# Two cross-attention layers in one kernel: an inverse root by Newton steps in place of a power, and a split issued two thirds of a slot earlier

## The chip, the cores and the metric

The kernel runs on one core of one Trainium2 chip. The metric is the device time of one execution in microseconds (us). The core has TensorE (PE in the profile, with its weight loads on a row of their own, PEld), VectorE (DVE), ScalarE (ACT), GpSimd (POOL) and SyncE (SP), which here only issues DMAs. Every engine works through its own queue in order.

## The reference

Sixteen sequences x of 256 positions by 320 channels pass through two cross-attention layers with 20 heads of 16 channels, against a context of 256 tokens by 512 channels. Both layers have text tokens, and a few image tokens whose attention gets an extra semantic term. The part of the second layer that the change touches:

```python
probs_t = jax.nn.softmax(scores_t, axis=-1)                    # text attention
qsem = jnp.einsum('bhst,bte->bhse', probs_t, text_ehs)         # mean text per head and position
qsem = _l2norm(qsem)                                           # x / max(|x|, 1e-12)
ip_n = _l2norm(ip_ehs)                                         # the 4 image tokens
sem = jnp.einsum('bhse,bne->bhsn', qsem, ip_n)
fused = attn_scores + 0.5 * sem
probs_ip = jax.nn.softmax(fused, axis=-1) * spatial_mask
ip_out = jnp.einsum('bhsn,bhnd->bhsd', probs_ip, v_ip)
out = (text_out + ip_out) @ W_out + b_out + residual
```

So for each position and head an inverse norm of `qsem` is wanted: 256 x 20 values in each batch.

## The kernel before

Everything is one unrolled program. It runs in *slots*: one slot is one group of four heads of one batch, five slots make a batch, slots 0 to 79 are layer 1 and slots 80 to 159 layer 2 (`NS` is 80). `slot1(k)` lists what TensorE does in a slot of layer 2, in order: scores and turned scores (`both1`: L894, L888), attention over the values (`attend1`: L948, and L958 for the norms), and the four steps of the norm's quadratic form (`norm1`: L936) of the slot before. Between them, at 0.33, 0.67 and 1.0 of the slot, `fill` runs side tasks whose due times have come. Each side task is a Python generator; the list of due times at its definition says at which slot each of its steps may be issued.

Matrices are split into a rounded high part and a low part, so that fast matmuls keep full precision. Four users of POOL matter here:

- `rounded1` (L926 on ACT, L927 on POOL): per slot four times, ACT rounds half of the attention weights P and POOL subtracts, 128 x 512 each. The result `wt` is multiplied by the norm's matmul (L937 on DVE) and summed by TensorE.
- `open1(b)`, with `split` and `project`: loads layer 1's output x of batch b (a DMA on SP into `xq`, one buffer), splits it (ACT L593 and L594, then POOL L595 and L596, tile `hq`, one buffer) and projects it to layer 2's queries (TensorE L606 and L609). The first matmul of L606 reads ACT's part, the second one reads POOL's. `open1(b)` has six due times relative to the batch's first slot n: load, split, then projection and its stores.
- `image_softmax(b)`: from the sums of `settle1` it makes the inverse norm (L1021, L1023, and the power at L1026, on POOL), the image scores (L1029, L1031), their maximum (L1034), exponential (L1038) and normalisation (L1044, L1046), then turns them over on DVE (L1053). `close1(b)` multiplies the result with the image values (TensorE L1063), and projects the output with its own split (tile `ho`, L595) and L606. For the last batch `image_softmax` runs in two parts: groups 0 to 3 (32 values per partition) and group 4 (8 values).
- `keys1` and `tokens1`: the split of the next context (L163) and small copies.

TensorE's order is pinned: it is the order in which the Python code issues matmuls. The other queues are ordered by a planner, which simulates the program with prices of its own and takes ready instructions by the order in which they were issued. `queued` adds a tie: the instruction isn't placed ahead of the last one that `anchor` marked on its engine. On ACT the anchors are the exponentials (L908), on POOL the subtractions (L927); the split of x (`hq`) is tied to both.

```python
    def queued(inst, *behind):
        for other in behind or [anchors.get(inst.ins.engine)]:
    ...
            anchor(nc.gpsimd.tensor_sub(W[k, u][:, t], P[k, u][:, t], f(R[k, u][:, t])))
    ...
        order = queued if tag == "hq" else lambda inst: inst
        order(eng.tensor_sub(hl[:, 3:5], src[:, 0:2], f(hl[:, 0:2])))
```

Of the kernel before, what the change touches and what calls it, by code (L numbers as in the profile page):

```python
# [11 lines left out]
ALU = mybir.AluOpType  # L12
# [9 lines left out]
CP = 384  # L22
# [8 lines left out]
NG = H // 4  # L31
# [11 lines left out]
def RAMP(t):  # L43
    return t if t < -5 or t > 3 else (t + 5) * 0.375
# [5 lines left out]
def xattn2(  # L50
# [27 lines left out]
    nc = tc.nc  # L78
    f = lambda ap: ap.bitcast(F32)
    mm = nc.tensor.matmul  # L80

    def dma(out, in_):
        nc.sync.dma_start(*(f(ap) if ap.dtype == FR else ap for ap in (out, in_)))
# [9 lines left out]
    whole = ps.tile([128, 1024], F32, tag="S0", name="S", bufs=1)  # L93
# [16 lines left out]
    def buf(tag, shape, dtype=F32, bufs=1, name=None):  # L110
        if tag in ("wB", "wD", "vr", "raw"):
            return sb.tile(shape, dtype, tag=tag, name=name or tag, bufs=bufs)
        size = 1
        for d in shape[1:]:
            size *= d
        if tag not in slots:
            slots[tag] = [0, dtype] + [const_tile([128, max(size, words.get(tag, 0))], f"{tag}_{i}", dtype) for i in range(bufs)]
        n, kind, *ring = slots[tag]
        assert kind == dtype and len(ring) == bufs, tag
        slots[tag][0] += 1  # L120
        t = ring[n % bufs][: shape[0], :size]
        names = "abcd"[: len(shape) - 1]
        if len(names) > 1:
            t = t.rearrange(f"p ({' '.join(names)}) -> p {' '.join(names)}", **dict(zip(names, shape[1:])))
        return t
# [305 lines left out]
    w1, v1t, gmt = {}, [], []  # L431
# [74 lines left out]
    def weights3():  # L506
        gm = buf("vr", [128, 3 * (H * V0W + 16)], FR, bufs=3, name="gm")
        gm = gm[:, : 7 * 128].rearrange("p (g n) -> p g n", n=128)
        nc.gpsimd.memset(f(gm), 0.0)
        gmt.append(gm)  # L510
        yield
        if len(gmt) == 2:
            one, two = [buf("rs", [128, 2 * S], bufs=2, name="one") for i in range(2)]
            w1["vb"], w1["mhalf"] = one[:, :CP], one[:, CP : CP + NG * 8]
            w1["pT"], w1["pip"] = two[:, :S], two[:, S:].rearrange("p (f c) -> p f c", c=32)
            nc.vector.memset(w1["mhalf"], -0.5)
            nc.gpsimd.memset(w1["pip"], 0.0)

    ct1, doubled = {}, {}
# [69 lines left out]
    def split(src, neg, eng, tag):  # L589

        hl = buf(tag, [128, 5, S], FR)
        order = queued if tag == "hq" else lambda inst: inst
        order(nc.scalar.copy(hl[:, 0:2], src[:, 0:2]))  # L593
        order(nc.scalar.activation(hl[:, 2], src[:, 2], AF.Copy, scale=neg))  # L594
        order(eng.tensor_sub(hl[:, 3:5], src[:, 0:2], f(hl[:, 0:2])))  # L595
        order(eng.tensor_add(hl[:, 2], src[:, 2], f(hl[:, 2])))  # L596
        return hl
# [15 lines left out]
    def queries(l, a):  # L613
        qh = buf("q", [128, 2, 3, S], FR)

        def evac(m, pp):
            evacuate(qh[:, 0, m], qh[:, 1, m], pp, m)

        qd = dram.tile([3, CH, S], F32, tag=f"qd{l}", name=f"qd{l}", bufs=2)
        steps = project(l, wq[l], a, evac)  # L620
        for m in range(2):
            next(steps)
            yield
        for r, s in ((0, 0), (1, 1), (2, 0)):
            dma(qd[r, :256].rearrange("(m p) t -> p m t", p=128), qh[:, s, :2])
        next(steps)
        for r, s in ((slice(0, 3, 2), 0), (slice(1, 2), 1)):
            to = qd[r, 256:].rearrange("r p t -> p r t")
            dma(to, qh[:64, s, 2].unsqueeze(1).to_broadcast(list(to.shape)))
        yield  # L630
        return qh, qd
# [4 lines left out]
    def load(src, tag):  # L636
        x = buf(tag, [128, 3, S])
        dma(x, src.rearrange("(k p) t -> p k t", p=128))
        return x
# [372 lines left out]
    def image_softmax(b, lo=0, hi=NG):  # L1012

        gs, n = slice(lo, hi), hi - lo
        nt, si = norms[b][:, gs], image[b]
        square = norms[b][:, lo + 1 : hi + 1, :, 5]
        pool = nc.gpsimd
        small = lambda n, t: buf(t, [128, NG, 8] + ([n] if n > 1 else []))[:, gs]

        u = small(1, "u")  # L1020
        pool.tensor_mul(u, nt[:, :, :, 0], nt[:, :, :, 0])  # L1021
        yield
        nc.vector.scalar_tensor_tensor(u, u, EPS2 / 4, square, op0=ALU.mult, op1=ALU.max)  # L1023
        yield
        r = small(1, "r")
        pool.tensor_tensor(r, u, w1["mhalf"].rearrange("p (f s) -> p f s", f=NG)[:, gs], op=ALU.pow)  # L1026
        b4 = lambda t: t.unsqueeze(3).to_broadcast([128, n, 8, NIP])
        a = small(NIP, "a")
        pool.tensor_mul(a, nt[:, :, :, 1:5], b4(r))  # L1029
        by_group = lambda t: t[:, :, : NG * NIP].rearrange("p f (g n) -> p g f n", n=NIP)[:, gs]  # L1030
        pool.tensor_add(a, a, by_group(si))  # L1031
        yield
        m4 = small(1, "m4")
        nc.vector.tensor_reduce(m4, a, axis=AX.X, op=ALU.max)  # L1034
        yield
        pool.tensor_sub(a, a, b4(m4))
        yield
        nc.scalar.activation(a, a, AF.Exp, scale=SCALE)  # L1038
        yield
        z4 = small(1, "z4")  # L1040
        nc.vector.tensor_reduce(z4, a, axis=AX.X, op=ALU.add)
        nc.vector.reciprocal(z4, z4)
        yield
        pool.tensor_mul(z4, z4, mk.unsqueeze(1).to_broadcast([128, n, 8]))  # L1044
        pi = w1["pip"]
        pool.tensor_mul(by_group(pi), a, b4(z4))  # L1046
        if hi < NG:
            return
        vb = w1["vb"]
        dma(vb, vipd[NIP * b : NIP * (b + 1)].unsqueeze(0).to_broadcast([32, NIP, CP]))  # L1050
        yield
        pT = w1["pT"]
        nc.vector.transpose(pT, pi.rearrange("p f c -> p (f c)"))  # L1053
        nc.gpsimd.tensor_mul(vb, vb, w1["bmask"])
        return pT, vb

    def close1(b):
        hT, (pT, bd) = results["gathered", 1, b], get("i1", b)

        def extra(hT):  # L1060
            for p in range(3):
                ip = bank()[:, :S]
                mm(ip, bd[:, p * 128 : (p + 1) * 128], pT, start=True, stop=True)  # L1063
                nc.vector.tensor_add(hT[:, p], hT[:, p], ip)
                yield

        y = yield from finish(1, b, hT, load(x1d[b], "xc"), extra)
        dma(out_d[b].rearrange("(k p) t -> p k t", p=128), y)
# [5 lines left out]
    def open1(b):  # L1074
        x = load(x1d[b], "xq")
        yield
        xs = split(x, tmask[:, 5:6], nc.gpsimd, "hq")
        yield
        get("w2")
        qh, qd = yield from queries(1, xs)  # L1080

        return qd
# [4 lines left out]
    def task(key, times, make, *needs):  # L1087
        tasks[key] = [times, 0, make, needs, len(tasks)]
# [14 lines left out]
    def get(*key):  # L1103
        while key not in results:
            step(key)
        return results[key]
# [20 lines left out]
    def shifted(n, *times):  # L1127

        return [RAMP(n + t) for t in times]
# [4 lines left out]
    for c in range(B // 2):  # L1134
        n, k = 10 * c, [("k0", c)] if c else []
# [11 lines left out]
    for b in range(B):  # L1147
        n = NS + 5 * b
        task(("k1", b), shifted(n, -7, -6.67, -6.33, -5.67, -5, -4.67), lambda b=b: keys1(b), ("w2",), *([("grams", b - 1)] if b else []), *([("w4", 1)] if b > 2 else []))
        task(("t1", b), shifted(n, -3.67, -3, -2.67, -2.33, -1.67), lambda b=b: tokens1(b), ("k1", b), ("w3", b % 2))  # L1150
        task(("o1", b), shifted(n, -7.67, -7, -6.67, -5.33, -4.33, -4), lambda b=b: open1(b), ("w7",), ("c0", b), *([("o1", b - 1)] if b else []))
        task(("i1", b), shifted(n, 6.67, 6.67, 6.67, 7.33, 7.33, 7.67, 7.67, 8, 8.33), lambda b=b: image_softmax(b, NG - 1 if b == B - 1 else 0), ("gathered", 1, b), ("taken", B + b - 1), *([("i1a",)] if b == B - 1 else []))
        task(("c1", b), shifted(n + (1.67 if b > B - 3 else 0), 8.67, 8.67, 8.67, 8.67, 9, 10.33, 11.67, 12.67), lambda b=b: close1(b), ("i1", b), ("w4", 1))
    task(("i1a",), [2 * NS + 0.1], lambda: image_softmax(B - 1, 0, NG - 1), ("i1", B - 2))
    spread = lambda t, d, n: [t + d * i for i in range(n)]
    thirds = lambda n, t: [t + i // 3 + (0.2, 0.6, 1.0)[i % 3] for i in range(n)]
# [4 lines left out]
    for i in range(2):  # L1161
        task(("w3", i), [NS - 4 + 5 * i], weights3)
# [147 lines left out]
```

## Time and profile before

| what | value |
|---|---|
| runs | 1537.6, 1539.21, 1541.0 us; median 1539.21 |
| profiled execution | 1533.3 us, of which the span from first to last instruction is 1531.5 |
| granted TensorE clock, mean | 0.982 |
| PE busy | 1439.7 us, 94% |
| POOL busy | 1263.5 us, 83% |
| DVE busy | 1116.6 us, 73% |
| ACT busy | 891.0 us, 58% |
| HBM traffic over the span | 127 GB/s |

Shares are means over two layers with different work. Layer 2 fills about the second half of the span; its batches repeat every 49.9 us. In timeline rows the first number is the start in us from the beginning of the span and the second the time that the group took; "x4" is the number of instructions, and brackets hold the engine's idle time before it and what ended it. L numbers are lines of the kernel.

### The profile page before, as it was taken

Reading aid. Unit: us, or ns where it says so; the run is one execution under the profiler, and the core shown is the slowest. Engines: PE = TensorE matmul, PEld = TensorE weight load, DVE = VectorE, ACT = ScalarE, POOL = GpSimd, SP = SyncE. Lnnn points to the kernel's source line nnn. Section 1 sums busy time; section 2 is a strip of 40 time slices with the busy share of each in tenths; the row PEclk is TensorE's granted clock in tenths of the full one; section 3 lists DMA queues with packets and bytes.
Section 4 is the critical chain, followed back from the end, with each engine's and each line's share of the span. In section 5 each row is a group of like instructions: output and inputs, shape, how many; then the busy total and the mean of one; then the engine's idle time right before and its main releaser. Section 6 shows DMA issues by size and latency. Waiting matters only on the chain.

```text
span 1531.5 us, 36088 instructions
## 1 busy us (share of the span) xinstructions
PE 1439.7 (94%) x12726; PEld 1162.6 (76%) x12726; DVE 1116.6 (73%) x2544; ACT 891.0 (58%) x2037; POOL 1263.5 (83%) x1325
## 2 busy tenths in 40 slices
PE   6789999999999999779999999999999999999996
PEld 5678878788888877657777777877777777777764
DVE  5466767676767677876787878777777877787874
ACT  5346555556565645545666666666656666666561
POOL 4269898889898986888688898888988898889796
PEclk9899999999999999999999999999999999999998
DMA  6766677677767675774444354444444344433311
GB/s 209 205 194 185 206 196 215 185 220 193 213 189 211 188 217 141 196 223 147 108 133 125 111 144 111 116 129 124 118 119 133 112 125 120 134 111 110 105 28 36
DMA packets 228815, 233.04 MB, mean 152 GB/s; under 512 B 38410, under 2 KB 198508, under 8 KB 228620
## 3 DMA queue, kind: packets, MB, share of 16 engines
q1 hardware_dynamic: 226428, 229.44, 53.0%
q8 instruction: 101, 1.65, 0.5%
q10 hardware_dynamic: 2208, 1.30, 0.3%
q14 instruction: 78, 0.64, 0.1%
HBM read 118.04 MB, written 77.10 MB: 127 GB/s over the span
## 4 chain that ended last, share of the span: by engine, by line
PE 69%; POOL 11%; DMA 8%; DVE 5%; ACT 3%; issue 2%; SPq 1%; ACTq 1%; POOLq 0%; DVEq 0%
PE X L936 14%; PE X L248 13%; PE X L606 6%; PE P L796 5%; PE P L948 4%; POOL wt L927 4%; PE S L739 4%; PE P L958 4%; PE T L763 3%; PE T L888 3%; PE S L894 3%; DMA ks<-M 2%; POOL P L769 2%; PE X L258 2%; PE X L609 2%
## 5 line engine op out<-in xcount | busy, mean ns | idle before, releaser
L769 POOL TENSOR_TENSOR P<-P,rs 128x512 f32<-128x512 f32 x320 | 408.1, 1299 | 91.3 <-ACT P L766 89.8
L927 POOL TENSOR_TENSOR wt<-P,ctb 128x512 f32<-128x512 f32 x320 | 405.8, 1292 | 68.1 <-ACT ctb L926 68.1
L936 PE MATMUL X<-ctb,gm 128*128 128x512 f32 x1120 | 305.3, 402 | 0.1
L766 ACT ACTIVATE P<-T 128x512 f32<-128x512 f32 x320 | 175.6, 594 | 151.1 <-PE T L763 107.9
L937 DVE TENSOR_TENSOR wt<-X,wt 128x512 f32<-128x512 f32 x320 | 216.7, 683 | 39.3 <-PE X L936 32.8
L908 ACT ACTIVATE P<-T 128x512 f32<-128x512 f32 x320 | 173.4, 594 | 80.0 <-PE T L888 77.5
L936 PEld LDWEIGHTS X<-ctb,gm 128*128 128x128 f32 x1120 | 196.1, 189 | 31.2 <-DVE wt L937 0.7
L926 ACT ACTIVATE ctb<-P 128x512 fp32r<-128x512 f32 x320 | 187.5, 627 | 22.9 <-PE X L936 21.7
L896 DVE TENSOR_REDUCE mn<-S 128x4 fp32r<-128x1008 f32 x160 | 191.6, 1197 | 0.0
L741 DVE TENSOR_REDUCE mn<-S 128x4 fp32r<-128x716 f32 x160 | 142.6, 891 | 0.0
L796 PE MATMUL P<-P,vr 128*32 128x256 f32 x1920 | 125.5, 391 | 4.7 <-POOL P L769 3.3
L739 PE MATMUL S<-ks,qs 125*128 125x256 f32 x640 | 117.2, 306 | 6.0 <-DMA qs<-tph 3.4
L739 PEld LDWEIGHTS S<-ks,qs 125*128 125x128 f32 x640 | 88.2, 194 | 40.9 <-issue 24.0
L1026 POOL TENSOR_TENSOR r<-u,rs 128x40 f32<-128x40 f32 (+2 forms) x17 | 108.8, 6397 | 3.9 <-DVE u L1023 3.8
L763 PE MATMUL T<-qs,ks 127*128 127x256 f32 x640 | 107.9, 290 | 4.0 <-ACT P L766 3.9
L740 DVE TENSOR_REDUCE mn<-S 128x4 fp32r<-128x308 f32 x160 | 74.4, 465 | 30.0 <-PE S L739 28.9
L763 PEld LDWEIGHTS T<-qs,ks 127*128 127x128 f32 x640 | 90.5, 194 | 7.3 <-ACT P L766 6.3
L796 PEld LDWEIGHTS P<-P,vr 128*32 128x32 f32 x1920 | 55.8, 111 | 46.2 <-issue 6.4
L606 PE MATMUL X<-hq,wE 128*128 128x256 f32 x512 | 80.6, 297 | 10.6 <-POOL hq L595 6.0
L807 DVE STREAM_TRANSPOSE nt<-P 128x512 f32<-128x512 f32 x80 | 57.0, 712 | 44.2 <-PE P L796 43.5
L606 PE MATMUL X<-ho,wF 128*128 128x256 f32 x512 | 75.3, 289 | 11.8 <-ACT mt L749 5.3
L948 PE MATMUL P<-P,v1t 128*32 128x256 f32 x1280 | 85.9, 386 | 0.0
(234 smaller groups left out, 3015.7 us busy)
## 6 DMA issues: line engine op xcount, KB each, us to landing
qd<-q SPq DMA_DIRECT2D x96, 256.0 KB
qs<-tph SPq DMA_DIRECT2D x64, 308.0 KB
rawc<-in_cT_dram SPq DMA_DIRECT2D x60, 256.0 KB
qs<-qd SPq DMA_DIRECT2D x80, 192.0 KB
ks<-kd SPq DMA_DIRECT2D x80, 192.0 KB
ks<-kd SPq DMA_DIRECT2D x160, 96.0 KB
qs<-qd SPq DMA_DIRECT2D x160, 96.0 KB
kd<-kst SPq DMA_DIRECT2D x57, 256.0 KB
```

What stands on the lines that cost most here:

```text
L248: last = mm(out, lhs(a, k), rhs(b, k), start=i == 0, stop=i == len(terms) - 1)
L606: mm(pp, w(s, k, m), a[:, t], start=i == 0, stop=i == len(terms) - 1)
L739: mm(sp[:, h], Q[: XROW + T0, h, t * 128 : (t + 1) * 128], K[: XROW + T0, h], start=True, stop=True)
L763: mm(st[p][:, j], K[:KS0, 2 * p + j, t * 128 : (t + 1) * 128], Q[:KS0, 2 * p + j], start=True, stop=True)
L766: exp = anchor(nc.scalar.activation(pt, st[p], AF.Exp, scale=SCALE))
L769: anchor(nc.gpsimd.tensor_mul(pt, pt, rs[:, t : t + 1].to_broadcast([128, 2, S])))
L796: mm(pv[32 * s : 32 * s + 32, o : o + S], v[:, vt, h : h + 32], P[k, s // 2][:, t, s % 2], start=vt < 2, stop=vt != 1,)
L896: anchor(nc.vector.tensor_reduce(maxes[k + 2][:, t], sp[:, :, :T1], axis=AX.X, op=ALU.max))
L926: nc.scalar.activation(R[k, u][:, t], P[k, u][:, t], AF.Copy, scale=0.5)
L927: anchor(nc.gpsimd.tensor_sub(W[k, u][:, t], P[k, u][:, t], f(R[k, u][:, t])))
L936: mm(yp, gm[:, gb], R[k, u][:, kt], start=i == 0, stop=i == len(blocks[n]) - 1)
L937: nc.vector.tensor_mul(W[k, u][:, n], yp, W[k, u][:, n])
```

## The change

The power `u ** -0.5` becomes a first value taken linearly from the bits of u, read as a whole number (0x5F3759DF minus half of it), and three Newton steps r := r (1.5 - 0.5 u r r). All thirteen instructions are on POOL; the scratch `e` lies in the buffer of `m4`, which is written later. The constant tile of -0.5 goes, with its memset. In the due times of `open1` the load moves from n - 7.67 to n - 8.33 and the split from n - 7 to n - 7.67, that is from the end of slot n-8 to its 0.33 mark; the projection's due times stay.

```diff
             one, two = [buf("rs", [128, 2 * S], bufs=2, name="one") for i in range(2)]
-            w1["vb"], w1["mhalf"] = one[:, :CP], one[:, CP : CP + NG * 8]
+            w1["vb"] = one[:, :CP]
             w1["pT"], w1["pip"] = two[:, :S], two[:, S:].rearrange("p (f c) -> p f c", c=32)
-            nc.vector.memset(w1["mhalf"], -0.5)
             nc.gpsimd.memset(w1["pip"], 0.0)
...
         r = small(1, "r")
-        pool.tensor_tensor(r, u, w1["mhalf"].rearrange("p (f s) -> p f s", f=NG)[:, gs], op=ALU.pow)
+        e = small(1, "m4")
+        whole = lambda t: t.bitcast(mybir.dt.int32)
+        pool.tensor_scalar(whole(r), whole(u), -0.5, 1597463007.0, op0=ALU.mult, op1=ALU.add)
+        for i in range(3):
+            pool.tensor_mul(e, r, r)
+            pool.tensor_mul(e, e, u)
+            pool.tensor_scalar(e, e, -0.5, 1.5, op0=ALU.mult, op1=ALU.add)
+            pool.tensor_mul(r, r, e)
...
-        task(("o1", b), shifted(n, -7.67, -7, -6.67, -5.33, -4.33, -4), lambda b=b: open1(b), ("w7",), ("c0", b), *([("o1", b - 1)] if b else []))
+        task(("o1", b), shifted(n, -8.33, -7.67, -6.67, -5.33, -4.33, -4), lambda b=b: open1(b), ("w7",), ("c0", b), *([("o1", b - 1)] if b else []))
```

## The prediction

> **What bounds the kernel now.** I read the page's busy shares first, then the busy time of each engine over one batch of layer 2 (windows), then TensorE's waits in layer 2, then the timeline around the one wait that is left, and last the chain of waits at the end. The page, with the group that the change replaces:
>
> ```profile
> PE 1439.7 (94%) x12726; PEld 1162.6 (76%) x12726; DVE 1116.6 (73%) x2544; ACT 891.0 (58%) x2037; POOL 1263.5 (83%) x1325
> ...
> L1026 POOL TENSOR_TENSOR r<-u,rs 128x40 f32<-128x40 f32 (+2 forms) x17 | 108.8, 6397 | 3.9 <-DVE u L1023 3.8
> ```
>
> The power costs POOL 108.8 us, but that is no price yet: POOL counts only where TensorE waits for it. One batch of layer 2, from one power to the next (window; busy time of PE, PEld, DVE, ACT, POOL, then the granted clock):
>
> ```profile
> 979.36:1029.27 49.91, 49.63 (x443) 38.76 (x442) 38.93 (x86) 31.69 (x71) 43.63 (x49) 1.00 0.44 122
> ```
>
> TensorE is recorded idle for 0.28 of 49.91 us; POOL has 6.3 us to spare. So TensorE sets the pace, and only what removes one of its waits can help. Its waits between 760 and 1500 us (total, times, longest):
>
> ```profile
> PE X L606 <- POOL hq L595: 4.2, 13, 0.5
> ...
> PE X L1063 <- DVE wt L937: 0.2, 1, 0.2
> ```
>
> One wait, once per batch: the query projection of layer 2 (`project`, L606) needs the low part of the split of x (`split`, L595), which POOL makes late. Thirteen batches have it, 0.32 us each by this count. The timeline shows a larger price. First the eight matmuls of the projection that waits, then eight that do not, then eight of the output projection after a short wait of their weight loads:
>
> ```profile
> 1000.02 0.36 PE L606 MATMUL X<-hq,wE 128*128 128x256 f32 x1
> 1000.67 1.20 PE L606 MATMUL X<-hq,wE 128*128 128x256 f32 x7 [0.28 <-POOL hq L595]
> 1001.71 1.78 PE L936 MATMUL X<-ctb,gm 128*128 128x512 f32 x7
> ...
> 1012.73 1.10 PE L606 MATMUL X<-hq,wE 128*128 128x256 f32 x8
> 1013.67 0.86 PE L936 MATMUL X<-ctb,gm 128*128 128x512 f32 x3
> ```
> ```profile
> 982.88 1.21 PE L606 MATMUL X<-ho,wF 128*128 128x256 f32 x8
> 983.93 0.86 PE L936 MATMUL X<-ctb,gm 128*128 128x512 f32 x3
> ```
>
> From the first L606 to the next group's first matmul: 1001.71 - 1000.02 = 1.69 us with the wait, 0.94 without (1013.67 - 1012.73), 1.05 after the short one. The wait therefore costs 0.64 to 0.75 us a batch, not 0.28: a matmul's recorded span covers the time in which the next could have started. [...] By the recorded idle the wait would be worth 4.2 us in all, by the starts 9.0; this trace, with 0.65 us from start to start and 0.28 recorded, sides with the starts.
>
> **The change part by part.**
>
> *The split moved.* Why is `hq` late? POOL in that batch, and the other engines around it:
>
> ```profile
> 979.36 6.77 POOL L1026 TENSOR_TENSOR r<-u,rs 128x40 f32<-128x40 f32 x1 [0.20 <-DVE u L1023]
> 986.10 5.03 POOL L927 TENSOR_TENSOR wt<-P,ctb 128x512 f32<-128x512 f32 x4
> 991.07 0.49 POOL L1029 TENSOR_TENSOR a<-tmp,r 128x160 f32<-128x160 f32 x1
> ...
> 993.55 2.56 POOL L927 TENSOR_TENSOR wt<-P,ctb 128x512 f32<-128x512 f32 x2 [0.42 <-ACT ctb L926]
> ...
> 996.06 0.27 POOL L1044 TENSOR_TENSOR z<-z,mk 128x40 f32<-128x40 f32 x1
> 996.41 0.47 POOL L1046 TENSOR_TENSOR rs<-a,z 128x160 f32<-128x160 f32 x1
> 996.84 2.52 POOL L927 TENSOR_TENSOR wt<-P,ctb 128x512 f32<-128x512 f32 x2
> 999.33 1.29 POOL L595 TENSOR_TENSOR hq<-xq,hq 128x512 fp32r<-128x512 f32 x1
> 1000.58 0.73 POOL L596 TENSOR_TENSOR hq<-xq,hq 128x256 fp32r<-128x256 f32 x1
> ```
> ```profile
> 989.56 1.09 ACT L908 ACTIVATE P<-T 128x512 f32<-128x512 f32 x2 [1.21 <-PE T L888]
> 990.54 0.62 ACT L593 CAST hq<-xq 128x512 fp32r<-128x512 f32 x1
> 991.05 0.52 ACT L594 ACTIVATE hq<-xq,tmask 128x256 fp32r<-128x256 f32 x1
> ...
> 998.11 0.43 DVE L1053 STREAM_TRANSPOSE rs<-rs 128x256 f32<-128x256 f32 x1
> 1001.34 0.38 SPq L83 DMA_DIRECT2D xq<-x1d  x1
> 1003.09 1.29 PEld L1063 LDWEIGHTS X<-rs,rs 128*128 128x128 f32 x6
> ```
>
> ScalarE's half of the split is done at 991.57; POOL's half starts 7.8 us later, because `queued` ties it behind the last subtraction (L927) issued before it, and at n-7 all four of slot n-8 have been issued (the pairs at 993.55 and 996.84). At n-7.67 the step runs before them, and its tie is the last of the four that begin at 986.10. So POOL can take it from 991.6 on and ends it near 993.6 (1.29 + 0.73), 6.4 us before the second L606 wants it. ScalarE's two instructions keep their tie, the exponentials at 989.56. What is pushed back: the pair at 993.55 by 0.1 to 0.6 us, and all four are used by the matmuls of the next slot (from 1001.71); from 999.33 on POOL is 2.0 us earlier. The load of x moves too, from n-7.67 to n-8.33. But SP issues it as soon as `xq` is free: 1001.34 is right behind the end of L596 (1001.31), and is the next batch's load, over four slots ahead of its step. It will follow L596 to about 993.6, earlier than now past SP's other transfers, which are issued slots ahead of use: nothing, and x arrives no later. If that cover failed, ScalarE's copies would wait for x and the 0.7 us would stay. For layer 1's last slots (the first two batches) no L606 wait is shown; nothing there.
>
> Value: 13 x 0.69 = 9.0 us gained (middle of 0.64 and 0.75; 8.3 to 9.8), and not less than 4.2 if only the recorded idle goes.
>
> *The power replaced.* One instruction becomes 13 on POOL: a `tensor_scalar` that reads and writes the bits as integers, and three rounds of three multiplications and a `tensor_scalar`, each fed by the one before. The nearest rows, and the memset that goes:
>
> ```profile
> L1021 POOL TENSOR_TENSOR u<-tmp 128x40 f32<-128x40 f32 x15 | 3.9, 263 | 1.1
> ...
> L1021 POOL TENSOR_TENSOR u<-tmp 128x8 f32<-128x8 f32 x1 | 0.2, 203 | 0.1
> ```
> ```profile
> L516 DVE MEMSET rs<- x1: 92/92/92, 677.8 to 677.8; 128x40 f32 x1
> ```
>
> A 40-wide product lasts 0.26 us, but a dependent pair (L1044, then L1046) starts 0.35 us apart: 13 x 0.35 = 4.5 us, against 986.10 - 979.36 = 6.74 for the power. The trace has no `tensor_scalar` with integers; bounds are 0.26 each (3.4 us: gaps filled by others) and 0.49, the 160-wide L1029 (6.4). I take 4.5, nearest to the row with a dependence. POOL gains 2.2 us a batch (0.3 to 3.3). On the path this is worth nothing in the steady part: the pair at 993.55 was waiting for ScalarE, which was waiting for TensorE, so `hq` behind it would be no earlier for a faster power; and with the split moved, the cover is the 6.4 us above. The memset's 0.09 us of DVE is nothing.
>
> *The end.* Here both powers are on the chain of waits, and widths are 32 and 8:
>
> ```profile
> 1505.13 4.25 POOL r L1026
> ```
> ```profile
> 1505.13 5.44 POOL L1026 TENSOR_TENSOR r<-u,rs 128x32 f32<-128x32 f32 x1 [0.87 <-DVE u L1023]
> 1510.54 1.26 POOL L595 TENSOR_TENSOR ho<-hT,ho 128x512 fp32r<-128x512 f32 x1
> ...
> 1514.09 1.65 POOL L1026 TENSOR_TENSOR r<-u,rs 128x8 f32<-128x8 f32 x1
> 1515.70 0.45 POOL L1031 TENSOR_TENSOR a<-a,si 128x128 f32<-128x128 f32 x1
> 1516.11 0.24 POOL L1029 TENSOR_TENSOR a<-tmp,r 128x32 f32<-128x32 f32 x1
> 1516.44 0.25 POOL L1031 TENSOR_TENSOR a<-a,si 128x32 f32<-128x32 f32 x1
> ```
>
> Now 5.41 + 1.61 = 7.0 us. Thirteen 32-wide steps at the dependent spacing of 1516.11 to 1516.44 (0.33): 4.3. Thirteen 8-wide ones at 0.20 + 0.07 = 0.27: 3.5. Sum 7.8, so 0.8 us lost. Bounds: gaps filled, 13 x (0.24 + 0.20) = 5.7 (1.3 gained); 0.35 for each, 9.1 (2.1 lost). [...]
>
> *Sum.* -9.0 + 0.8 = -8.2 us. The profiled execution took 1533.3 us (span 1531.5 and 1.8 around it) and would take 1525.1; the runs have a median of 1539.2, 5.9 above that execution, and I set the sum against the median: **1531.0 us**. Own range of this case: 8.3 to 9.8 gained, 1.3 gained to 2.1 lost at the end, so 1528.1 to 1533.0.
>
> **The rivals.**
>
> *The recorded idle is all there is to win*, or TensorE takes up another small wait in the same place: 13 x 0.32 = 4.2, less 0.8 at the end: 1535.8. For it: windows show 0.28 us of idle per batch. Against: the 1.69 against 0.94 us above.
>
> *The split doesn't move on POOL.* The tie says only what it must not precede; the planner orders POOL by its own clock. If it leaves `hq` behind the second pair, nothing is won: 1540.0. For it: the planner already issues loads four slots away from their step. Against: the operands are ready at 991.57, the first pair's only at 993.55, and the step is issued first.
>
> *The Newton chain is spread out and the image path comes late (slower).* The planner fills gaps between dependent instructions with other ready POOL work, as it did here, where a pair of subtractions stands between L1044 and L1046:
>
> ```profile
> 796.05 0.28 POOL L1044 TENSOR_TENSOR z<-z,mk 128x40 f32<-128x40 f32 x1
> 796.28 2.54 POOL L927 TENSOR_TENSOR wt<-P,ctb 128x512 f32<-128x512 f32 x2
> ```
>
> From L1029 to the end of L1053 are 7.5 us (991.07 to 998.54), and L1063 loads its result at 1003.09, or 1002.3 once TensorE is 0.75 earlier. L1029 must start by 994.8, 15.5 us after the first step; the chain itself needs 4.5, so it decides from 11.0 us of foreign work on, nearly nine subtractions of 1.26. All 12 gaps filled: 4.5 + 15.1 = 19.6, so 4.1 us late in 13 batches, +53 - 9.0 + 0.8: 1584. For it: 12 such gaps. Against: in those 15.5 us POOL has six subtractions, not nine.
>
> **How the numbers follow.** The forecast has 0.61, the recorded idle only 0.14, no move on POOL 0.14, the late image path 0.11. A measurement of this kernel tells about 0.2% (3.1 us) from no change. The first rival's 3.4 us lies on that edge: half counts as faster. Faster 0.61 + 0.07 = 0.68, same 0.07 + 0.14 = 0.21, slower 0.11. The range reaches from 1527 (the own range and 1 us of run scatter; the runs go from 1537.6 to 1541.0) to 1541 (the second rival and 1 us); outside are the slower case and a rest on the fast side.
>
> **What would show it.** Split: L595 of `hq` starts near 991 to 992 in the corresponding batch, the row L606 from POOL `hq` is gone from TensorE's waits, the eight L606 take about 1 us, and the batch 49.2 instead of 49.9 us. Newton: 13 instructions within 5 to 12 us, POOL's busy time some 34 us lower (15 x 2.2). End: from the first Newton step of width 32 to the last of width 8 about 0.8 us more. Wrong would be: a batch of 49.9 us, a new row in TensorE's waits (L1063 from L1053 above all), or a Newton step above 0.5 us.

## The result, and the profile after

The changed kernel takes 1528.79 us (median of 15 runs, 1524.48 to 1537.15), against 1537.6 us for the kernel before in the same comparison (15 runs, 1534.06 to 1547.4). The ratio is 0.9936, 95% interval 0.9915 to 0.9958: faster by 0.4 to 0.9%. The forecast was 1531.0 us, and "faster". The profiled spans are 1531.5 and 1524.7 us, so 6.8 us less in these two executions.

The total came out about right, but its parts did not. (Line numbers of the changed kernel are one lower than those of the kernel before up to the root, and six higher behind it: L936 is now L935, L1063 is L1069. The kernels e2, e3, e8 and e10 below are numbered like the changed kernel, e1 and e4 like the kernel before.) Both programs issue the same 12726 matmuls in the same order, so a matmul of the one can be laid against the same matmul of the other, and the time between two of them compared:

| stretch between the same matmuls | before, us | after, us | difference | forecast |
|---|---|---|---|---|
| start to 755 us (layer 1, first slots of layer 2) | 755.22 | 755.94 | +0.72 | 0 |
| thirteen batches of layer 2 (one, then twelve) | 48.85 + 600.02 | 47.20 + 595.86 | -1.65 - 4.16 | -9.0 |
| the last slots before the end's first stage | 87.16 | 87.39 | +0.23 | 0 |
| the end, three stages | 40.25 | 38.31 | -1.94 | +0.8 |

The first line holds layer 1, which the change touches only by a memset and by the splits for the first batches of layer 2; over the eleven profiled executions of this study, which issue the same matmuls there, it lies between 753.1 and 761.6 us, so 0.72 says nothing. Of the first batch's 1.65 us, 0.93 is the wait for `hq` and 0.60 a wait of the image product (L1063). The steady part gave less than forecast, and the end gained where a loss was forecast.

The page of the changed kernel, its busy row:

```profile
PE 1436.7 (94%) x12726; PEld 1159.4 (76%) x12726; DVE 1114.5 (73%) x2543; ACT 891.4 (58%) x2037; POOL 1209.5 (79%) x1529
```

POOL is 54 us less busy. That fits the groups: one power group of 108.8 us went, and the Newton groups together are 54.8 us. They are these (groups by line; the last columns are busy us, mean ns of one, idle before):

```profile
L1032 POOL TENSOR_TENSOR r<-r,m 128x40 f32<-128x40 f32 (+2 forms) x51 | 13.5, 265 | 3.8
L1030 POOL TENSOR_TENSOR m<-m,u 128x40 f32<-128x40 f32 (+2 forms) x51 | 13.5, 265 | 3.8
L1029 POOL TENSOR_TENSOR m<-r 128x40 f32<-128x40 f32 (+2 forms) x51 | 12.7, 248 | 3.8
L1031 POOL TENSOR_SCALAR m<-m 128x40 f32<-128x40 f32 (+2 forms) x51 | 11.3, 222 | 4.0
...
L1027 POOL TENSOR_SCALAR r<-u 128x40 int32<-128x40 int32 (+2 forms) x17 | 3.8, 222 | 3.6 <-DVE u L1022 3.5
```

Eight whole batches of layer 2, from the same matmul to the same matmul (window; span, then busy time of PE, PEld, DVE, ACT, POOL, then the granted clock). Before, then after:

```profile
842.06:1241.24 399.18, 396.72 (x3531) 310.00 (x3530) 311.86 (x681) 253.43 (x561) 349.19 (x386) 1.00 0.44 123
```
```profile
841.39:1237.49 396.10, 395.97 (x3531) 308.57 (x3529) 308.19 (x681) 254.33 (x562) 321.16 (x481) 1.00 0.44 124
```

399.18 / 8 = 49.90 us a batch has become 396.10 / 8 = 49.51: 0.39 us gained, not 0.69. Yet the split does what was forecast. POOL and TensorE of the changed kernel in the batch that answers to the one shown in the prediction (timeline; start, duration):

```profile
977.59 0.22 POOL L1027 TENSOR_SCALAR r<-u 128x40 int32<-128x40 int32 x1 [0.20 <-DVE u L1022]
977.90 0.25 POOL L1029 TENSOR_TENSOR m<-r 128x40 f32<-128x40 f32 x1
...
981.58 0.27 POOL L1032 TENSOR_TENSOR r<-r,m 128x40 f32<-128x40 f32 x1
981.81 1.29 POOL L926 TENSOR_TENSOR wt<-P,ctb 128x512 f32<-128x512 f32 x1
...
990.19 1.30 POOL L594 TENSOR_TENSOR hq<-xq,hq 128x512 fp32r<-128x512 f32 x1
```
```profile
998.48 1.19 PE L605 MATMUL X<-hq,wE 128*128 128x256 f32 x8
999.51 1.80 PE L935 MATMUL X<-ctb,gm 128*128 128x512 f32 x7
```

The thirteen steps take 981.81 - 977.59 = 4.22 us, with nothing between them. `hq` starts 12.6 us after the first step; before, it started 20.0 us after the power's start (999.33 - 979.36). The eight matmuls that wait for it now take 999.51 - 998.48 = 1.03 us from start to start instead of 1.69. So this wait is gone in full, and something else took part of the gain back. Between 760 and 1500 us the rows of PE (first fence) show nothing of it; it stands only among the waits of the weight loads (PEld, second fence), in a row that the kernel before doesn't have:

```profile
PE T L887 <- DMA qs<-mt: 1.4, 1, 1.4
PE X L608 <- DVE wt L936: 0.4, 1, 0.4
PE X L935 <- DVE hT L1070: 0.2, 1, 0.2
```
```profile
PEld X L935 <- PE X L935: 5.3, 13, 0.4
```

The new one stands once per batch in a group of seven norm matmuls, at its fourth. The group and the matmul after it, before and after:

```profile
991.74 1.79 PE L936 MATMUL X<-ctb,gm 128*128 128x512 f32 x7
...
993.37 0.75 PE L609 MATMUL X<-ho,wF 128*128 128x256 f32 x5
```
```profile
989.95 2.04 PE L935 MATMUL X<-ctb,gm 128*128 128x512 f32 x7
991.82 0.75 PE L608 MATMUL X<-ho,wF 128*128 128x256 f32 x5
```
```profile
990.79 0.76 PEld L935 LDWEIGHTS X<-ctb,gm 128*128 128x128 f32 x4 [0.42 <-PE X L935]
```

1.63 us became 1.87. What else happens there: ScalarE takes the image exponential (L1044) ahead of the slot's second pair of exponentials (L907), and VectorE stands waiting for it:

```profile
988.21 0.34 ACT L1044 ACTIVATE a<-a 128x160 f32<-128x160 f32 x1 [1.65 <-POOL a L1042]
988.45 1.07 ACT L907 ACTIVATE P<-T 128x512 f32<-128x512 f32 x2
...
990.33 0.35 ACT L915 CAST mt<-X 4x256 fp32r<-4x256 f32 x1
```
```profile
988.58 0.32 DVE L1047 TENSOR_REDUCE z<-a 128x40 f32<-128x160 f32 x1 [0.75 <-ACT a L1044]
...
989.48 1.20 DVE L895 TENSOR_REDUCE mn<-S 128x4 fp32r<-128x1008 f32 x1
990.59 0.68 DVE L936 TENSOR_TENSOR wt<-X,wt 128x512 f32<-128x512 f32 x1
```

In the kernel before, the exponential came at 993.88, after the group. The shorter root brought the image path forward, and so into a place where it is in the way. There are two candidates for what it delays: ScalarE's copy of the maxima (L915), or VectorE's reduction of the scores and the first norm product behind it (L895, L936). Each of them empties a tile that matmuls filled, and so frees its place for later matmuls.

### The profile page after: what moved, and what is told of

It is laid out like the page before. It is cut to its first block, busy times and chain, and to the rows that moved or that the text cites. A ratio compares the mean times of both kernels' runs of the same rounds, so it can differ in the third digit from the quotient of the medians.

```text
span 1524.7 us, 36323 instructions
## 1 busy us (share of the span) xinstructions
PE 1436.7 (94%) x12726; PEld 1159.4 (76%) x12726; DVE 1114.5 (73%) x2543; ACT 891.4 (58%) x2037; POOL 1209.5 (79%) x1529
## 3 DMA queue, kind: packets, MB, share of 16 engines
q8 instruction: 102, 1.67, 0.5%
## 4 chain that ended last, share of the span: by engine, by line
PE 75%; DVE 6%; DMA 6%; POOL 6%; ACT 2%; issue 2%; SPq 1%; ACTq 1%; POOLq 0%; DVEq 0%
PE X L935 16%; PE X L248 14%; PE X L605 6%; PE P L795 6%; PE P L947 5%; PE S L738 5%; PE P L957 4%; PE T L887 3%; PE S L893 3%; PE T L762 3%; DMA rawc<-in_cT_dram 2%; POOL P L768 2%; PE X L608 2%; PE X L564 2%; PE X L258 2%
## 5 line engine op out<-in xcount | busy, mean ns | idle before, releaser
L935 PE MATMUL X<-ctb,gm 128*128 128x512 f32 x1120 | 308.0, 402 | 0.5 <-DVE hT L1070 0.2
L936 DVE TENSOR_TENSOR wt<-X,wt 128x512 f32<-128x512 f32 x320 | 216.2, 680 | 45.9 <-PE X L935 43.3
L935 PEld LDWEIGHTS X<-ctb,gm 128*128 128x128 f32 x1120 | 194.5, 189 | 36.3 <-PE X L935 5.3
L907 ACT ACTIVATE P<-T 128x512 f32<-128x512 f32 x320 | 172.9, 593 | 63.7 <-PE T L887 60.2
L895 DVE TENSOR_REDUCE mn<-S 128x4 fp32r<-128x1008 f32 x160 | 191.4, 1196 | 0.0
L957 PE MATMUL P<-wt,zone 128*32 128x256 f32 x1280 | 84.2, 379 | 0.0
L605 PE MATMUL X<-hq,wE 128*128 128x256 f32 x512 | 75.7, 291 | 6.6 <-ACT hq L592 4.0
```

Source lines behind the costliest of these rows:

```text
L605: mm(pp, w(s, k, m), a[:, t], start=i == 0, stop=i == len(terms) - 1)
L895: anchor(nc.vector.tensor_reduce(maxes[k + 2][:, t], sp[:, :, :T1], axis=AX.X, op=ALU.max))
L935: mm(yp, gm[:, gb], R[k, u][:, kt], start=i == 0, stop=i == len(blocks[n]) - 1)
L936: nc.vector.tensor_mul(W[k, u][:, n], yp, W[k, u][:, n])
```

## The experiments

The table gives, for the same eight batches, the time per batch, and the means from start to start of the three places where the kernels differ: the eight query projections that use `hq`; the group of seven norm matmuls; and the eight matmuls of the next slot's second half of scores (four turned, four plain). The three columns together give the difference of the batch times to within 0.05 us, so nothing larger is left untold.

| kernel | batch | eight projections | seven norm matmuls | eight scores matmuls |
|---|---|---|---|---|
| before | 49.90 | 1.71 | 1.62 | 0.67 |
| after | 49.51 | 1.03 | 1.88 | 0.67 |
| e1, due times only | 49.48 | 1.03 | 1.62 | 0.92 |
| e4, no tie | 49.46 | 1.03 | 1.62 | 0.91 |
| e2, Newton only | 49.87 | 1.37 | 1.92 | 0.67 |
| e3, exponential tied | 49.27 | 1.03 | 1.62 | 0.67 |
| e7, exponential after the rounding | 49.25 | 1.03 | 1.62 | 0.67 |
| e10, sum tied | 49.35 | 1.04 | 1.62 | 0.81 |
| e8, six rounds | 50.17 | 1.03 | 1.62 | 1.58 |
| e5, power for the last root | 49.55 | 1.03 | 1.91 | 0.67 |
| e9, e7 and e5 together | 49.25 | 1.03 | 1.62 | 0.67 |

**One part alone: the due times (e1).** The kernel before, with the power kept and the new due times of `open1`:

```diff
-        task(("o1", b), shifted(n, -7.67, -7, -6.67, -5.33, -4.33, -4), ...
+        task(("o1", b), shifted(n, -8.33, -7.67, -6.67, -5.33, -4.33, -4), ...
```

> The kernel before with the due times moved, the power kept. Theory A (the moved split takes away TensorE's wait for hq, and the Newton steps bring a new wait of 0.27 us a batch by putting the image exponential ahead of the slot's exponentials on ScalarE): L606's wait for hq gone, no new wait, a batch of 49.2 to 49.3 us, 8 to 9 us faster than before up to 1490 us, the end as before: ratio near 0.994. Rival B (both parts share the gain, the split is only early enough with a faster POOL): a batch of 49.5 or more.

Measured: 1533.86 us, ratio 0.9953 (0.9931 to 0.9976). The wait for `hq` goes, but the batch is only 0.42 us shorter: 49.48 us lies between theory A's 49.2 to 49.3 and rival B's 49.5. Something small is given back here too, in another place. With the power kept, `hq` now stands on POOL ahead of the image path's subtraction L1036; the image exponential and then the image sum on VectorE come later, and with the sum the reduction of the next slot's scores (L896) behind it. POOL, VectorE and TensorE's weight loads of this kernel:

```profile
995.79 1.32 POOL L595 TENSOR_TENSOR hq<-xq,hq 128x512 fp32r<-128x512 f32 x1
...
997.76 0.49 POOL L1036 TENSOR_TENSOR a<-a,m 128x160 f32<-128x160 f32 x1
```
```profile
998.65 0.32 DVE L1041 TENSOR_REDUCE z<-a 128x40 f32<-128x160 f32 x1 [0.30 <-ACT a L1038]
...
1000.97 1.20 DVE L896 TENSOR_REDUCE mn<-S 128x4 fp32r<-128x1008 f32 x1
```
```profile
1002.28 0.33 PEld L894 LDWEIGHTS S<-ks,qs 48*128 48x128 f32 x4
```

The reduction empties the tile S that the plain scores fill next. In each of the eight batches their weight loads start 0.11 or 0.12 us behind its end (here 1002.17 and 1002.28); in the changed kernel 0.26 us lie between the two, so there they don't wait for it. The scores take 0.92 us instead of 0.67. What follows: the late `hq` is worth 0.68 us a batch, and with the power kept the move gives 0.25 of that back through POOL's queue.

**The tie (e4).** The kernel before with its old due times, and only POOL's two instructions of this split left free of `queued`:

```diff
-        order(eng.tensor_sub(hl[:, 3:5], src[:, 0:2], f(hl[:, 0:2])))
-        order(eng.tensor_add(hl[:, 2], src[:, 2], f(hl[:, 2])))
+        (eng.tensor_sub(hl[:, 3:5], src[:, 0:2], f(hl[:, 0:2])))
+        (eng.tensor_add(hl[:, 2], src[:, 2], f(hl[:, 2])))
```

> The kernel before, with its power and its old due times, where only POOL's half of the split of x is no longer tied behind the last subtraction (ScalarE's half stays tied). Tests the prediction's reason for hq being late. Theory A (the tie holds it back): L595 of hq starts right after ScalarE's half, 7 to 8 us earlier than before, no L606 wait for hq, and the batch as in the run with the due times alone, 49.4 to 49.5 us. Rival B (POOL's backlog from the power holds it back): hq within 2 us of where it was, the wait stays, a batch of 49.9.

Measured: one run, 1531.49 us, beside a median of 1541.58 for the kernel before; the batch as in e1, 49.46 us. So it was the tie that held `hq` back, and the new due time does no more than put the split ahead of the subtractions that it would be tied to. Moving the load of x has no part in it: with the split moved and the load left where it was, the planner gives the same instructions in the same order on every engine, so there is no other kernel to measure.

**The other part alone: Newton (e2).** The changed kernel with the old due times.

```diff
-        task(("o1", b), shifted(n, -8.33, -7.67, -6.67, -5.33, -4.33, -4), ...
+        task(("o1", b), shifted(n, -7.67, -7, -6.67, -5.33, -4.33, -4), ...
```

> The Newton steps with the old due times. Theory A: the wait for hq stays, shorter (POOL runs the four subtractions ahead of hq without a pause), about 0.4 us of the 0.7; the new wait of the norm's matmuls (0.25 to 0.3 us) is there: a batch of 49.7 to 49.95 us, so within 3 us of the kernel before up to 1490 us, 0 to 1 us gained at the end; ratio 0.997 to 1.000. Rival B: a batch of 49.5, half the gain.

Measured: 1535.54 us, ratio 0.9969 (0.9946 to 0.9992). TensorE's waits, PE and then PEld:

```profile
PE X L605 <- POOL hq L594: 1.1, 2, 0.9
```
```profile
PEld X L935 <- PE X L935: 5.9, 13, 0.5
```

In the steady part the root is not worth nothing, as forecast: it moves `hq` forward by 0.34 us a batch (1.71 to 1.37) and puts the norm group back by 0.30 (1.62 to 1.92), and the two cancel. So the new wait belongs to Newton, not to the moved split. What e2 gains, it gains at the end, below.

**The exponential out of the way (e3 and e7).** Two versions of the changed kernel that hold the image exponential back: e3 behind the last exponential of the slot, e7 behind the last rounding of P.

```diff
-        nc.scalar.activation(a, a, AF.Exp, scale=SCALE)
+        queued(nc.scalar.activation(a, a, AF.Exp, scale=SCALE))
```

> The changed kernel with the image exponential tied behind the slot's exponentials, as hq is; it then stands on ScalarE after hq's two instructions and still ahead of the copy of the maxima (mt). Tells which instruction holds the norm's matmuls up. If it is ScalarE's copy of the maxima: it ends about as late as now, the wait stays at 0.2 to 0.3 us, a batch of 49.5. If it is VectorE (the reduction behind the reciprocals): the wait goes, a batch of 49.2 to 49.3.

```diff
+    rounds = []
...
-            nc.scalar.activation(R[k, u][:, t], P[k, u][:, t], AF.Copy, scale=0.5)
+            rounds[:] = [nc.scalar.activation(R[k, u][:, t], P[k, u][:, t], AF.Copy, scale=0.5)]
...
-        nc.scalar.activation(a, a, AF.Exp, scale=SCALE)
+        queued(nc.scalar.activation(a, a, AF.Exp, scale=SCALE), *rounds)
```

> The changed kernel with the image exponential tied behind ScalarE's roundings of P, where it stood in the kernel before. Theory A: the new wait goes, the hq wait stays away: a batch of 49.2 to 49.3 us, 3 to 4 us faster than the changed kernel, ratio to the kernel before near 0.991 to 0.992. Rival C (the lost 0.3 us a batch is something else that the Newton steps bring, such as POOL or port contention): still 49.5.

Measured: e3 1526.19 us, ratio 0.9905 (0.9875 to 0.9935); e7 1526.48 us, ratio 0.9912 (0.988 to 0.9944). In both the group of seven is back at 1.62 us and the batch at 49.27 and 49.25: 0.63 to 0.65 us under the kernel before, which is nearly the 0.69 of the forecast. TensorE is then busy without a recorded gap; the same eight batches in e7:

```profile
841.00:1235.03 394.03, 394.03 (x3530) 309.20 (x3529) 309.54 (x681) 254.35 (x561) 321.11 (x481) 1.00 0.45 124
```

The early exponential is the cause of the new wait. But holding it back relieves ScalarE and VectorE alike (in e3 the copy of the maxima, too, starts earlier against the group than in the changed kernel), so the batch times of these two runs don't say which of them passes the delay on.

**ScalarE or VectorE (e10).** The changed kernel, with the exponential left ahead on ScalarE, and only VectorE's sum of it tied behind the slot's second reduction:

```diff
-        nc.vector.tensor_reduce(z4, a, axis=AX.X, op=ALU.add)
+        queued(nc.vector.tensor_reduce(z4, a, axis=AX.X, op=ALU.add))
```

> The changed kernel, with only VectorE's sum of the image exponentials tied behind the slot's second reduction of scores; the exponential itself stays on ScalarE where the change put it, ahead of the slot's second exponentials. Theory V: the new wait of 0.25 to 0.27 us in the norm group comes from VectorE, whose sum waits 0.75 us for that exponential with the reduction and the first norm product queued behind it; the group's fourth matmul takes the bank that this product empties. Then the wait is gone, the group of seven takes 1.63 us again, twelve batches take about 592 to 593 us, ratio about 0.991. Theory S: it comes from ScalarE, whose copy of the maxima is late behind the exponential; then the row stays at 5.3 us for 13, the group at 1.87 us, twelve batches at 595 to 596 us, ratio about 0.9936.

Measured: 1524.5 us, ratio 0.9939 (0.9907 to 0.9971), the batch 49.35 us. The timelines of ScalarE, VectorE and TensorE in the batch that answers to those above:

```profile
985.15 0.34 ACT L1044 ACTIVATE a<-a 128x160 f32<-128x160 f32 x1 [1.67 <-POOL a L1042]
```
```profile
985.31 1.20 DVE L895 TENSOR_REDUCE mn<-S 128x4 fp32r<-128x1008 f32 x1
986.43 0.31 DVE L1047 TENSOR_REDUCE z<-a 128x40 f32<-128x160 f32 x1
986.65 0.68 DVE L936 TENSOR_TENSOR wt<-X,wt 128x512 f32<-128x512 f32 x1
```
```profile
986.86 1.79 PE L935 MATMUL X<-ctb,gm 128*128 128x512 f32 x7
988.49 0.75 PE L608 MATMUL X<-ho,wF 128*128 128x256 f32 x5
```

The exponential is still in front on ScalarE, whose copy of the maxima starts 0.41 us behind the group's start (987.27), as late as the 0.38 us in the changed kernel (990.33); and the group takes 1.63 us all the same. So it was VectorE: while it stood 0.75 us for the image sum, what stood behind it in its queue was late. In the changed kernel the last of the scores that the reduction reads have their recorded end at 987.98 (L893), the sum starts at 988.58 and the reduction only at 989.48; its end, 990.68, lies 0.73 us behind the group's start, here (986.51) 0.35 us ahead of it.

Theory V names the first norm product as what the fourth matmul waits for. That is one instruction too far: in the changed kernel the product's recorded end, 991.27, lies after the fourth matmul's start, 990.82. It is the reduction ahead of the product. It ends at 990.68, and the fourth matmul's weight load starts at 990.79. Over the eight batches this distance is 0.11 to 0.12 us each time, in the changed kernel, in e2 and in e5, the three kernels where the group is slow; in all the others it is 0.82 or 0.83 us. The program that the kernel builds to has the same: the planner put the tile X of the fourth matmul in the place of the scores that the reduction reads, and the matmul's wait on VectorE is for this reduction.

Of e3's gain e10 keeps all but 0.1 us a batch, and that is in the scores, 0.81 instead of 0.67, whose weight loads here, too, start 0.12 us behind a reduction. The eight batches answer to theory V in all but the instruction; the whole run (0.9939) can't tell the two theories apart, since both forecasts lie in its interval.

**Is the chain's length free? (e8).** The changed kernel with six rounds in place of three: twelve more instructions for the same root.

```diff
-        for i in range(3):
+        for i in range(6):
```

> The changed kernel with six Newton rounds in place of three: twelve more POOL instructions, 3.9 us more POOL time in each batch, the same result to rounding. Theory A (POOL's time is covered in the batches, and what costs 0.27 us a batch in the changed kernel is that its shorter chain brings the image exponential ahead of the slot's exponentials on ScalarE): the exponential falls back behind them, the wait of the norm's matmuls goes, a batch of 49.2 to 49.3 us although POOL works more; 2 to 6 us lost at the end. Rival B (POOL's time counts): a batch of 49.6 or more. Rival D, the prediction's slower case: the image path comes late for L1063, with a TensorE wait of over 1 us a batch.

Measured: 1553.53 us, ratio 1.0084 (1.0059 to 1.011): some 25 us slower than the changed kernel. Three windows of this kernel: the first batch, the eight batches, and the end's middle stage:

```profile
758.46:813.51 55.05, 48.09 (x423) 36.58 (x423) 40.23 (x89) 33.75 (x77) 42.48 (x71) 0.97 0.44 123
852.62:1253.96 401.34, 396.22 (x3530) 310.33 (x3529) 309.47 (x681) 255.30 (x561) 343.23 (x576) 1.00 0.43 122
...
1518.14:1537.36 19.22, 6.88 (x47) 4.83 (x47) 7.23 (x20) 1.57 (x4) 14.97 (x58) 0.81 0.18 52
```

Against the changed kernel: 7.9 us in the first batch (55.05 and 47.20), 0.66 us in each of the others (50.17 and 49.51), 3.8 us in the stage before it and 4.8 in this one (19.22 and 14.38). Theory A is half right: the norm group is back at 1.62 us, but the batch isn't at 49.2 to 49.3. The waits say why. TensorE, then VectorE in a steady batch:

```profile
PE S L893 <- DVE mn L895: 7.7, 12, 0.7
PE X L1069 <- DVE rs L1059: 7.0, 1, 7.0
```
```profile
1007.65 0.32 DVE L1040 TENSOR_REDUCE m<-a 128x40 f32<-128x160 f32 x1 [1.19 <-POOL a L1037]
```

In the first batch the image product L1069 itself comes 7 us late, and the granted clock over the batch is 0.97 where the changed kernel has 1.00 (755.94 to 803.14 us), 3.3 us at half the clock by estimate, which would be most of the remaining 0.9 us: this is the prediction's slower rival, a Newton chain with subtractions in its gaps, and it does occur once the chain is twice as long. In the steady batches L1069 is in time, but VectorE stands 1.19 us for POOL with the scores reduction behind it, and the scores take 1.58 us. So three rounds are short enough and six are not, and what gives way first is not the last user of the chain but the queue of the engine in between.

**The end: a power where it is cheap (e5), and both together (e9).** e5 is the changed kernel with the power kept for the last group's root, 8 values wide (the constant tile and its memset come back with it); e9 adds the tie of e7.

```diff
+        if n == 1:
+            pool.tensor_tensor(r, u, w1["mhalf"].rearrange("p (f s) -> p f s", f=NG)[:, gs], op=ALU.pow)
...
-        for i in range(3):
+        for i in range(3 if n > 1 else 0):
```

> The changed kernel with the power kept for the last 8-wide root alone. Theory A (the 8-wide chain of thirteen is on the path at the end): from the first 32-wide step on POOL to the last batch's L1063 matmul 1.5 to 2.5 us less than the changed kernel's 14.1 us. Rival B (its steps lie in the gaps of the other chain): 0 to 0.5 us less, or more. The batches stay at 49.5 to 49.6 us in both; the whole within 3 us of the changed kernel.

> The changed kernel with the image exponential tied behind the last rounding of P (as in e7) and the power kept for the 8-wide root alone (as in e5). The two touch different stages, so their gains should add. From the first matmul at 755 us to the end e7 took 765.4 us. Twelve batches (804 to 1404) should again take about 592 us, no wait of the norm group on TensorE. If the end's saving of e5 is real (13.2 us between the last two image products, against 14.4 with the Newton chain), the end is 1.2 us shorter and the ratio to before about 0.990. Rival: e5's shorter end was only where the half-clock pieces fell; then the ratio is e7's, about 0.991, and the two ends differ by no more than one such piece moves (1.3 to 1.9 us).

Measured: e5 1528.68 us, ratio 0.9923 (0.9898 to 0.9947); e9 1525.42 us, ratio 0.9925 (0.9897 to 0.9954). The end in three stages, from the last wait for a transfer to the image product of the next to last batch, from there to that of the last batch, and from there to the end. Before, e4, after and e5:

```profile
1491.25:1505.01 13.76, 12.56 (x97) 7.83 (x97) 7.52 (x17) 4.71 (x9) 10.68 (x15) 0.88 0.00 1
1505.01:1519.71 14.70, 7.88 (x47) 5.91 (x47) 7.20 (x21) 1.48 (x4) 12.94 (x16) 0.88 0.11 40
1519.71:1531.50 11.79, 6.09 (x27) 4.49 (x27) 3.13 (x7) 1.12 (x2) 1.96 (x2) 0.80 0.21 67
```
```profile
1491.00:1503.23 12.23, 11.02 (x98) 7.16 (x98) 7.54 (x17) 4.70 (x9) 10.85 (x15) 1.00 0.01 1
```
```profile
1486.39:1497.24 10.85, 10.85 (x97) 7.34 (x98) 6.10 (x13) 4.48 (x8) 8.55 (x11) 1.00 0.01 2
1497.24:1511.62 14.38, 6.58 (x48) 4.72 (x46) 8.02 (x23) 1.57 (x4) 11.20 (x40) 0.91 0.22 68
1511.62:1524.70 13.08, 7.54 (x27) 5.95 (x27) 3.14 (x7) 1.12 (x2) 1.95 (x2) 0.63 0.09 31
```
```profile
1496.42:1509.58 13.16, 6.59 (x47) 4.73 (x46) 7.88 (x23) 1.57 (x4) 10.54 (x28) 0.88 0.26 75
```

The first stage must be compared at the same clock: e4, which has the power but a clock of 1.00 there, takes 12.23 us, the changed kernel 10.85, so the shorter root is worth 1.38 us; e2, which has the Newton steps but the old due times, takes 10.86 at the same clock. The other 1.53 us to the kernel before are its clock of 0.88. In the second stage the change gains 0.32 us, and the power kept for eight values another 1.22 (13.16; e9 13.15), which lies between theory A's 1.5 to 2.5 and rival B's 0 to 0.5. In the third stage the work is the same, and the changed kernel loses 1.29 us at a clock of 0.63 against 0.80. So e5's saving is real in its stage; in the whole run neither it nor e9 can be told from the changed kernel, and e9 misses the 0.990 that it was expected to reach. One reason is in the profiled executions: the first batch of layer 2 takes 48.82 us in e5 and 49.20 in e9, where the changed kernel takes 47.20. There two products of VectorE (L163) last 2.23 and 2.28 us instead of 1.07, and the scores wait some 1.5 us for VectorE. e4 shows the same (2.32 us), the other kernels don't; why is open. The fastest ratio, e3's 0.9905, has an interval (up to 0.9935) that overlaps the changed kernel's (from 0.9915): a version better than the change is shown by the batch (0.24 to 0.26 us, over thirteen batches 3.1 to 3.4 us), not by the whole time.

## Why the prediction was right, and where it was not

*The price of the wait: right.* Pricing it by starts (0.64 to 0.75 us) and not by the recorded idle (0.28) was the step that carried the sum. The eight projections went from 1.71 to 1.03 us on the mean, 0.68. The rival "recorded idle only" falls. Its other half, that TensorE takes up another small wait, came true in part, in another group of matmuls.

*Why `hq` was late: right.* The tie was the cause (e4), the split moved on POOL as said, and the load's move did nothing. The rival "the split doesn't move on POOL" falls.

*What the moved split would be worth: the wait as priced, the net too small.* The wait for `hq` itself gave 9.1 us over the thirteen batches (0.93 and twelve times 0.68), as "13 x 0.69 = 9.0 us" has it. But the term took for granted that nothing else was near to binding. Only 0.39 us a batch came, and 5.8 us over the thirteen batches of the first table. What is missing is mainly the 0.26 us of the new wait in the norm group, and e10 shows its way: POOL's root earlier, image exponential earlier, VectorE's sum queued earlier and waiting, the reduction behind it late, and a norm matmul waiting for the reduction. Without that wait (e3, e7) the batch gains 0.63 to 0.65 us. With the power kept (e1) the split alone would have been short too, by the 0.25 us of the scores.

*The root in the steady part: the step that failed.* The prediction costed the faster power at nothing there and named the 6.4 us of room behind `hq` as its cover. That asked only what the root's lateness could delay. It didn't ask what its earliness would put in front of other work: the planner places ready instructions, so a chain that takes 4.2 us instead of 6.7 gets other places on ScalarE and VectorE. And the reason given for the unmoved split, that a faster power would bring `hq` no earlier, was wrong too: in e2 it took 0.34 us off the projections. The sign that the prediction named for being wrong, a new row in TensorE's waits, did appear, though only among the weight loads.

*Its length: right.* Forecast 4.5 us for the thirteen, measured 4.22. The expected drop of POOL's busy time was wrong, 34 us against 54: the 0.35 us from start to start was used, but 0.22 to 0.27 of it is busy time.

*The end: wrong sign.* Forecast +0.8 us. The 8-wide root went as the working has it, a loss, though smaller: 1.22 us by e5 against 3.5 - 1.6 = 1.9, since part of its steps run in the gaps of the 32-wide ones. From the first 32-wide step to the end of the last 8-wide one POOL takes 10.84 us (1497.49 to 1508.33), against 10.61 for the two powers (1505.13 to 1515.74): 0.2 us longer, not 0.8. An 8-wide step is hardly shorter than a wide one, 0.20 us against 0.22 to 0.27 for 40 values (L1027 to L1032 of the changed kernel), so thirteen of them keep POOL busy for 2.6 us where the one power took 1.65. What was missed is the first stage: there the kernel before waits 1.21 us for the image path of the next to last batch, and the prediction's list of waits ends at 1500 us:

```profile
1505.01 0.48 PE L1063 MATMUL X<-rs,rs 128*128 128x256 f32 x1 [1.21 <-DVE rs L1053]
```

With the Newton steps this wait is gone, and that is most of the 1.38 us. So a place where the length of the 40-wide power was on TensorE's path lay five microseconds behind the window's edge.

*The sum: right by luck.* -8.2 us was forecast; the medians differ by 8.8. In the traces from the first batch of layer 2 to the end it is -7.5: -5.8 in the batches, +0.2, and -1.9 at the end (of which -1.7 is the work of the first two stages, and the rest what the granted clock gave in the first stage and took in the third). Two errors, 3.2 us too much in the batches and 2.7 too little at the end, nearly cancelled. The slower rival didn't happen with three rounds, but e8 shows its mechanism at six.

## What to carry to other kernels

When a chain gets shorter, look not only at who waited for its end but at every instruction that it will now place earlier in an in-order queue: the first one that isn't quite ready holds back all that stands behind it (above, VectorE's image sum for 0.75 us). Price a wait of a busy engine from start to start of its instructions, and compare two versions matmul by matmul; in a window, 0.25 us of waiting a batch can hide in a busy share of 100% (395.97 of 396.10 us above). Read the waits to the end of the span, since the last batch has other limits than the steady ones.

## What the runs showed of the hardware

The granted clock at the end doesn't follow the length of TensorE's wait alone. In the first stage TensorE waits once for the same transfer in every version. In the kernel before (wait 1.67 us) the granted clock then falls to a half for 3.41 us and the stage takes 13.76 us; in e4 (1.51 us) and after (1.44 us) it doesn't fall, and in e7, where the wait was longer, 1.78 us, it doesn't either. Such a piece costs 1.53 us here (13.76 against e4's 12.23), as much as what the change does at the end.

The traces say more if each is laid on the grid of 3.41 us that the later half-clock pieces of the same trace mark (in the kernel before they start at 1513.03 and 1519.86 us, six and eight times 3.41 us behind the one at 1492.55). Where the clock fell, 1.49 us or more of TensorE's recorded idle time lay within one step of that grid, the step just before the fall: 1.67 us in the kernel before, 1.53 in e1, 1.98 in e9, 1.49 in e10. Where it didn't fall, the wait was cut by the grid (after 0.30 and 1.14, e4 1.15 and 0.36, e7 0.89 and 1.03 us) or shorter (e2 1.45, e5 1.44, e8 0.38). e3 alone doesn't fit, with 1.50 us in one step and no fall. So in ten of the eleven traces the fall goes with 1.49 us or more of idle time within one step; no run was made to test this.
